# Products with the values in tiles of 64 rows by 32 columns, summed from two banks

## The chip, the cores and the metric

The kernel runs on one core of a Trainium2 chip. The metric is device time in microseconds (us), launch to end, as the median of several executions. The engines that matter here are TensorE (PE; its weight loads are shown as PEld), VectorE (DVE), ScalarE (ACT), GpSimd (POOL) and SyncE (SP), which issues most DMAs. Each engine works through its own queue in order. TensorE writes to PSUM, which has eight banks of 128 partitions by 512 float32 values; ScalarE and VectorE read the results there.

## The reference

One block of a diffusion transformer in float32, on 16 sequences of 256 tokens of width 256, with 16 heads of 16 values each:

```python
x_norm = modulate(_ln(x), shift_a, scale_a)
q, k, v = jnp.split(x_norm @ W_qkv + b_qkv, 3, axis=-1)        # 16 heads of 16
attn_w = softmax(einsum('bhqd,bhkd->bhqk', q, k) * scale, axis=-1)
attn_out = einsum('bhqk,bhkd->bhqd', attn_w, v)
x = x + gate_a * (attn_out @ W_proj + b_proj)
q_c = _ln(x) @ W_qc + b_qc                                      # cross attention,
k_c, v_c = split(_ln(context) @ W_kvc + b_kvc, 2)               # keys and values of the context
x = x + attention(q_c, k_c, v_c) @ W_cproj + b_cproj
h = gelu(modulate(_ln(x), shift_m, scale_m) @ W_mlp1 + b_mlp1)
x = x + gate_m * (h @ W_mlp2 + b_mlp2)
```

The context has 256 tokens too. The change touches the second product of each attention, weights times values (`bhqk,bhkd->bhqd`), over 256 keys.

## The kernel before

The attention is cut into 32 *units*: a self attention ("s") or a cross attention ("c") of one sequence. The first four units are s, then mostly one of each in turn. The loop at lines 1084 to 1096 goes over the units n, and inside each over eight steps k (`beat`, line 947). A step works on several units at once: while unit n has its softmax weights made, unit n+1 gets its first scores, units n+2 and n+3 get their queries, keys and values, and units n-1 to n-3 are finished. An instruction's place in its engine's queue is the place of its call in the program (`InOrder`, line 40, keeps all engines to it). After the loop comes the MLP.

One step of the loop, in PE's order:

- `visit` (line 932). Four products `s` give scores of unit n+1, with queries along the partitions; DVE takes their maxima over the keys (`mx`, `s_tile`, line 603). They go to the two banks `sp`, of which there is one pair, so the next step's `s` has to wait for this step's `mx`. Then four products `st` give the scores of unit n again, turned, with the keys along the partitions (`t_part`, line 626); ACT makes the weights `pt` from them (`exp`, line 638). Row 63 of each half holds the negative maximum, so no subtraction is needed. These products use 63 or 64 rows of the array and all 128 columns, and those of the two row halves alternate.
- In odd steps, `lanes` (line 374): two projections, interleaved product by product, one on the upper and one on the lower 64 rows. Their results lie in the long bank pair (tag "gen", two buffers).
- In even steps, what stands in `beat` for that step. Steps 0 and 4 hold what is changed here.

Step 0 (line 978) and step 4 (line 1020), in order:

- `m_part` (line 615): PE turns the maxima of one half of a unit (`psm`), ACT makes them negative (`m`), and SP sends them by DMA into row 63 of the queries, to be read four steps later.
- `exps`: ACT's exponentials of this step.
- `av_part`, twice (line 657): the products with the values, tile `o`. Each call has eight products: two chunks c of 128 keys, four heads h. A product has 128 rows (the keys) and 32 columns of the array (the 16 values of a head, then columns of ones, which give the sum of the weights), and streams 256 queries. The four heads stand in the four column strips of the array (`tile_position=(0, h * 32)`). The two calls fill one bank; then ACT copies it to `oT` in SBUF (in the last call of all, DVE does).
- then in step 4 `p1.aT.turn`: PE turns the attention output A of the unit before (`psT_a`), and ACT reads it; in step 0 nothing more on PE.
- on DVE then the low parts of keys or queries (`q2.K.low` with tile `l_k` or `l_kc`, `q2.Q.low` with `l_q` or `l_qc`), which read a bank of the long pair, and, in every second unit, statistics for a layer norm: `st_c` in step 0, `st_s` in step 4.

`psm`, `o`, `psT` and the transposed `oT` (`psA`) share the short bank pair (tag "tr", two buffers in turn, `ps_gen`, line 68). A new use of a buffer waits until all reads of the old one are done. All eight banks are given out: two `sp`, two `st`, two long, two short.

A float32 product of this kind appears in the trace as two matmul instructions.

Of the kernel before, what the change touches and what calls it, by code (L numbers as in the profile page):

```python
# [10 lines left out]
F32 = mybir.dt.float32  # L11
F32R = mybir.dt.float32r
AF = mybir.ActivationFunctionType
ALU = mybir.AluOpType
AX = mybir.AxisListType

P = 128
# [4 lines left out]
def pixart_block(  # L22
# [8 lines left out]
    B, N, H = x.shape  # L31
# [3 lines left out]
    NT = N // P  # L35
# [21 lines left out]
    PE = InOrder(nc.tensor, True)  # L57
    ACT, DVE, POOL, SP = (InOrder(e, True) for e in (nc.scalar, nc.vector, nc.gpsimd, nc.sync))

    const = ctx.enter_context(tc.tile_pool(name="const", bufs=1))  # L60
    work = ctx.enter_context(tc.tile_pool(name="work", bufs=2))
# [3 lines left out]
    LONG, SHORT = "gen", "tr"  # L65
    ps_turn = [0]

    def ps_gen(name, tag=None):


        if tag is None and ps_turn[0] is not None:
            ps_turn[0] ^= 1
            tag = (SHORT, LONG)[ps_turn[0]]
        tag = tag or SHORT
        return psum.tile([P, 512], F32, tag=tag, name=name, bufs=2)
# [314 lines left out]
    def lanes(x, y):  # L390


        if x:
            x.ps, x.fresh = ps_gen(f"ps_{x.name}", LONG), True
        return zip_longest(*(lane(o, half) for half, o in enumerate((x, y)) if o))

    def run(steps, n=12):
        for _ in islice(steps, n):
            pass
# [82 lines left out]
    def load(u):  # L482
        if u.kind == "s":
            load_x(u.b)
        else:
            u.ct = work.tile([P, NT, H], F32, tag="c", name=f"c_{u.b}")
            SP.dma_start(u.ct, tok(ctxt, u.b))
# [129 lines left out]
    def m_part(u, hf):  # L617

        pst = ps_gen(f"psm_{u.n}_{hf}", SHORT)
        PE.transpose(pst[:16, :P], u.mx[:, hf].rearrange("p r a t -> p (r a t)"), ident)  # L620
        m = work.tile([16, P], F32R, tag="m", name=f"m_{u.n}_{hf}", bufs=1)
        ACT.mul(m, pst[:16, :P], -1.0)
        for par in range(2):
            SP.dma_start(u.q[par * 64 + 63:par * 64 + 64, 4 * hf:4 * hf + 4, :].bitcast(F32),
                         m[par * 8:(par + 1) * 8].bitcast(F32))
# [19 lines left out]
    def exps():  # L645

        for f in later:
            f()
        later.clear()
# [4 lines left out]
            for f in pieces:  # L654
                next(f)

    def av_part(u, g):

        if g % 2 == 0:
            u.po = ps_gen(f"o_{u.n}_{g}", SHORT).rearrange("p (g n) -> p g n", g=2)  # L660
        for c in range(NT):
            for h in range(4):
                par, pair = g % 2, g // 2 * 4 + h
                PE.matmul(u.po[h * 32:(h + 1) * 32, g % 2], u.v[:, c, par * 8 + pair], u.pt[pair][:, par, c],
                          start=(c == 0), stop=(c == NT - 1), tile_position=(0, h * 32))
        if g % 2 == 1:
            oT = work.tile([P, 2, N], F32, tag="oT", name=f"oT_{u.n}_{g}")
            last = u.n == nu - 1 and g == 3
            (DVE.tensor_copy if last else ACT.copy)(oT.rearrange("p g n -> p (g n)"),
                                                    u.po.rearrange("p g n -> p (g n)"))  # L670
            u.oT.append(oT)


    seq = [("s", b) for b in range(4)]
# [5 lines left out]
    for n, (kind, b) in enumerate(seq):  # L680
        u = Box()
# [5 lines left out]
    nu = len(units)  # L687
# [241 lines left out]
    def unit(n):  # L929
        return units[n] if 0 <= n < nu else None  # L930

    def visit(n, k, home=sp):


        v, e = unit(n + 1), k
        s = []
        if v:
            s = [s_tile(v, e // 2, par, e % 2, par, home) for par in range(2)]
        if n < 0:
            in_turn(*s)  # L940
            return
        t = [t_part(units[n], k, par) for par in range(2)]
        in_turn(*s)
        in_turn(*t)
        later.append(lambda: exp(units[n], k))

    def beat(n, k):
        if n < 0:
            visit(n, k, (st, sp)[k % 2])
            return  # L950
        cur, prev, nxt = unit(n), unit(n - 1), unit(n + 1)
        q2, q3, q4 = (v if v and v.n >= m else None
                      for v, m in zip(map(unit, (n + 2, n + 3, n + 4)), (1, 2, 3)))
        p1, p2, p3 = (v and v.post for v in map(unit, (n - 1, n - 2, n - 3)))
        whole = n > nu - 4
        if n - 2 > nu - 5:
            p2 = None
        if n - 3 > nu - 5 or p3 and p3.hurry:
            p3 = None
        q3T = q3  # L960
        lc = q4 if q4 and q4.kind == "c" else None
        ls = q4 if q4 and q4.kind == "s" else None
        lx = q3 if q3 and q3.kind == "c" else None
        late = lx and lx.b in (0, 1, B - 2, B - 1)
        early = lc if lc and lc.b not in (0, 1, B - 2, B - 1) else None
        if k == 0 and q2:
            q2.K.high()
            q2.K.send_high()
        if k == 2 and p2:
            p2.end()  # L970
        if k == 4 and q2:
            q2.Q.high()
            q2.Q.send_high()
        if k == 6 and q2:
            q2.V.keep()
        light = k == 6 and nxt and 0 <= n < nu - 4 and not lx
        visit(n, k, (sp[:, 0], ps_gen("s1", SHORT)) if light else sp)
        if k == 0:
            if cur:
                m_part(cur, 1)  # L980
            exps()
            if prev:
                av_part(prev, 2)
                av_part(prev, 3)
            if q2:
                q2.K.low()
                q2.K.send_low()
            if p3:
                p3.add()
            if ls and n > 0:  # L990
                load(ls)
            if lc:
                lc.ln[0].steps[0]()
            if p1:
                p1.gate()
        elif k == 1:
            exps()
            run(lanes(q2 and q2.Q, p2))
            if lc:
                lc.ln[0].steps[1]()  # L1000
                lc.ln[0].steps[2]()
        elif k == 2:
            exps()
            if prev:
                p1.turn(1)
            if q3T:
                q3T.T[0].turn()
                q3T.T[0].high()
            if prev:
                p1.norm(1)  # L1010
            if p2 and p2.hurry:
                p2.add()
        elif k == 3:
            exps()
            if q3T and q3T.kind == "s":
                q3T.T[0].low()
            run(lanes(q2 and q2.V, q2 and q2.Q))
            if q3T and q3T.kind == "c":
                q3T.T[0].low()
        elif k == 4:  # L1020
            if nxt:
                m_part(nxt, 0)
            exps()
            if cur:
                av_part(cur, 0)
                av_part(cur, 1)
            if prev:
                p1.aT.turn()
                p1.aT.high()
            if q2:  # L1030
                q2.Q.low()
                q2.Q.send_low()
            if p3:
                p3.store()
            if late:
                for f in lx.ln[1].steps:
                    f()
            if ls and not late:
                ls.ln[0].steps[0]()
                ls.ln[0].steps[1](False)  # L1040
        elif k == 5:
            exps()
            run(lanes(q3 and q3.K, q2 and q2.V))
            if prev:
                p1.aT.low()
            if ls and late:
                for f in ls.ln[0].steps:
                    f()
            elif ls:
                ls.ln[0].pow()  # L1050
                ls.ln[0].steps[2]()
            if early:
                early.ln[1].steps[0]()
            v = unit(n + 5)
            if v and v.kind == "c":
                load(v)
        elif k == 6:
            exps()
            if cur:
                cur.post.begin()  # L1060
                cur.post.turn(0)
            if lx:
                lx.T[1].turn()
                lx.T[1].high()
            if early:
                early.ln[1].steps[1]()
                early.ln[1].steps[2]()
            if prev and whole:
                p1.proj(0)
                p1.proj(1)  # L1070
        elif k == 7:
            exps()
            run(lanes(None if whole else p1, q3 and q3.K))
            if prev and whole:
                p1.end()
                p1.add()
                p1.store()
            if cur:
                cur.post.norm(0)
            if lx:  # L1080
                lx.T[1].low()
# [13 lines left out]
                for f in at_end[n - nu, q]:  # L1095
                    f()
    last = units[-1]
    av_part(last, 2)
    av_part(last, 3)
    o = last.post  # L1100
    pst = iter([lambda: o.turn(1), lambda: o.norm(1),
                lambda: (o.aT.turn(), o.aT.high()), o.aT.low,
# [76 lines left out]
```

## Time and profile before

| | us |
|---|---|
| median of 3 runs | 808.84 (808.31 to 809.41) |
| span of the profiled execution | 807.9 |
| PE busy | 782.7 (97%) |
| DVE busy | 597.5 (74%) |
| ACT busy | 585.0 (72%) |
| POOL busy | 465.6 (58%) |

The first products with the values start at 46.9 us, the last end at about 612 us; from there on it is the MLP. The profiled execution's own time is known by its span, from the first to the last instruction; the measured times include what lies around it.

A row of a group gives the engine, the operation, the tiles (written <- read), the shape, the count, the busy time in us, the mean duration of one in ns, and after the second bar the engine's idle time before these instructions and what ended it. A row of the timeline gives the start in us from the start of the span, the length in us, the engine, the operation, the tiles and the count of merged instructions. Shapes of products are rows*columns of the array, then partitions x elements of what is streamed. Matmuls are pipelined: the recorded length of one is its latency, and several are under way at once. Nearly all instructions have line 51, that of a helper, so they are told apart by their tiles.

### The profile page before, as it was taken

The numbers are of one execution on the slowest core, as the hardware profiler recorded it, in microseconds if no ns is written. First come the engines' busy times: TensorE is split into PE (matmuls) and PEld (weight loads), VectorE is DVE, ScalarE is ACT, GpSimd is POOL, SyncE is SP. The second block draws the span as 40 slices with busy tenths as digits, with TensorE's granted clock in tenths as the row PEclk, the third lists the DMA queues.
The fourth block names the chain that finished last, engine by engine and source line by source line (L and its number), as shares of the span: only waits on it lengthen the run. The fifth ranks groups of instructions, "written<-read, shape, count | busy, mean of one in ns | idle before, by whom it ended". The sixth has DMA issues, their size and how long they took to land.

```text
span 807.9 us, 23702 instructions
## 1 busy us (share of the span) xinstructions
PE 782.7 (97%) x9455; PEld 659.8 (82%) x9455; DVE 597.5 (74%) x1061; ACT 585.0 (72%) x1024; POOL 465.6 (58%) x405
## 2 busy tenths in 40 slices
PE   9999999999999999999999999999889999999997
PEld 8677777878878878877777777777568999999997
DVE  4887878788887888888788888777663666566662
ACT  3367888878888888878888878887556666666663
POOL 5745737575463756636475676563435666666653
PEclk9999999999999999999999999999999999999999
DMA  6553443435344453534445453534211313312211
GB/s 201 140 166 105 122 134 111 125 99 145 106 130 110 133 136 104 146 104 128 109 126 156 124 152 109 157 94 127 88 42 41 92 50 69 79 53 67 80 41 52
DMA packets 89938, 87.88 MB, mean 109 GB/s; under 512 B 9506, under 2 KB 85572, under 8 KB 89828
## 3 DMA queue, kind: packets, MB, share of 16 engines
q1 hardware_dynamic: 89364, 85.58, 37.7%
q8 instruction: 75, 1.23, 0.6%
q0 software_dynamic: 192, 0.52, 0.2%
q14 instruction: 35, 0.29, 0.1%
q10 hardware_dynamic: 272, 0.26, 0.1%
HBM read 26.97 MB, written 8.46 MB: 44 GB/s over the span
## 4 chain that ended last, share of the span: by engine, by line
PE 73%; DVE 10%; ACT 5%; POOL 5%; issue 5%; DMA 2%; SPq 0%; POOLq 0%; ACTq 0%
PE s L51 15%; PE o L51 13%; PE ph L51 11%; PE st L51 11%; DVE mx L51 7%; PE ps_qc L51 3%; ACT pt L51 3%; PE ps_q L51 3%; PE ps_kc L51 3%; PE ps_P_s L51 2%; PE ps_v_s L51 2%; PE psm L51 1%; PE ps_v_c L51 1%; PE ps_k L51 1%; PE ps_P_c L51 1%
## 5 line engine op out<-in xcount | busy, mean ns | idle before, releaser
L51 DVE TENSOR_REDUCE mx<-s 128x4 f32<-128x1024 f32 (+1 forms) x265 | 309.1, 1171 | 96.5 <-PE s L51 93.8
L51 ACT ACTIVATE pt<-st 128x1024 f32<-128x1024 f32 x256 | 261.1, 1020 | 46.5 <-PE st L51 39.8
L51 PE MATMUL s<-big 63*128 63x256 f32 x1008 | 120.7, 309 | 9.5 <-DVE mx L51 6.4
L51 PE MATMUL o<-pt,v 128*32 128x256 f32 x2048 | 123.8, 382 | 0.0
L51 POOL TENSOR_TENSOR hl<-hf,hh 128x512 fp32r<-128x512 f32 x64 | 88.5, 1392 | 56.0 <-ACT hh L51 55.6
L51 PEld LDWEIGHTS s<-big 63*128 63x128 f32 x1008 | 80.2, 185 | 44.6 <-DVE mx L51 22.5
L51 PE MATMUL st<-big 64*128 64x256 f32 (+1 forms) x1040 | 110.7, 284 | 4.0 <-ACT pt L51 3.9
L51 PEld LDWEIGHTS o<-pt,v 128*32 128x32 f32 x2048 | 60.0, 109 | 40.8
L51 PEld LDWEIGHTS st<-big 64*128 64x128 f32 (+1 forms) x1040 | 83.4, 186 | 9.2 <-ACT pt L51 7.1
L51 ACT ACTIVATE hf<-ph,bT 128x256 f32<-128x256 f32 x120 | 50.6, 475 | 27.8 <-PE ph L51 27.8
L51 ACT ACTIVATE hh<-ph,bT 128x256 fp32r<-128x256 f32 x120 | 50.5, 472 | 24.9 <-PE s L51 13.1
L51 ACT COPY oT<-o 128x512 f32<-128x512 f32 x63 | 37.0, 587 | 42.4 <-PE o L51 42.4
L51 POOL TENSOR_TENSOR xTl_c<-y_c,xTh_c 128x512 fp32r<-128x512 f32 x16 | 20.5, 1282 | 61.1 <-PE s L51 51.9
L51 POOL TENSOR_TENSOR xTl_as<-y_as,xTh_as 128x512 fp32r<-128x512 f32 x16 | 20.5, 1279 | 57.8 <-ACT y_as L51 57.8
L51 PE MATMUL ph<-wqch,wself 128*128 128x256 f32 x256 | 51.8, 285 | 0.0
L51 PE MATMUL ph<-wkch,wself 128*128 128x256 f32 x256 | 51.8, 286 | 0.0
L51 POOL TENSOR_TENSOR xTl_ac<-y_ac,xTh_ac 128x512 fp32r<-128x512 f32 x16 | 20.5, 1281 | 54.0 <-ACT y_ac L51 50.0
L51 PE MATMUL s<-big,hh 128*128 128x256 f32 x256 | 47.4, 282 | 0.0
L51 PE MATMUL st<-big,hh 128*128 128x256 f32 x256 | 47.2, 281 | 0.0
L51 DVE TENSOR_SCALAR xn_m<-x,mv_m,rs_m 128x256 f32<-128x256 f32 x32 | 38.2, 1235 | 11.4 <-POOL rs_m L51 11.4
L51 PEld LDWEIGHTS ph<-wqch,wself 128*128 128x128 f32 x256 | 42.0, 191 | 0.4 <-issue 0.4
L51 PEld LDWEIGHTS ph<-wkch,wself 128*128 128x128 f32 x256 | 41.9, 191 | 0.4
(222 smaller groups left out, 2380.9 us busy)
## 6 DMA issues: line engine op xcount, KB each, us to landing
big<-h_kc SPq DMA_DIRECT2D x64, 128.0 KB
big<-h_qc SPq DMA_DIRECT2D x64, 128.0 KB
big<-h_k SPq DMA_DIRECT2D x62, 128.0 KB
big<-h_q SPq DMA_DIRECT2D x62, 128.0 KB
big<-l_k SPq DMA_DIRECT2D x32, 128.0 KB
big<-l_q SPq DMA_DIRECT2D x32, 128.0 KB
c<-in_ctx_dram SPq DMA_DIRECT2D x16, 256.0 KB
g<-gd SPq DMA_DIRECT2D x16, 256.0 KB
```

Of the source, the lines that this page charges most:

```text
L51: i = f(*a, **k)
```

## The change

`av_part` with its two calls becomes `av_pair`. A chunk of 128 keys is cut into two halves of 64 rows. The products of the upper half of each chunk are summed in one bank, those of the lower half in another; each product has 64 rows and 32 columns, and there are 32 calls in a block where there were 16. Both buffers of the short pair are used. On the way out ACT copies the first bank to `oT`, and DVE adds the second to it, in place. In steps 0 and 4, `exps` and `av_pair` stand ahead of `m_part`, where `m_part` came first. The call behind the loop changes likewise.

```diff
-    def av_part(u, g):
-        if g % 2 == 0:
-            u.po = ps_gen(f"o_{u.n}_{g}", SHORT).rearrange("p (g n) -> p g n", g=2)
-        for c in range(NT):
-            for h in range(4):
-                par, pair = g % 2, g // 2 * 4 + h
-                PE.matmul(u.po[h * 32:(h + 1) * 32, g % 2], u.v[:, c, par * 8 + pair], u.pt[pair][:, par, c],
-                          start=(c == 0), stop=(c == NT - 1), tile_position=(0, h * 32))
-        if g % 2 == 1:
-            oT = work.tile([P, 2, N], F32, tag="oT", name=f"oT_{u.n}_{g}")
-            last = u.n == nu - 1 and g == 3
-            (DVE.tensor_copy if last else ACT.copy)(oT.rearrange("p g n -> p (g n)"),
-                                                    u.po.rearrange("p g n -> p (g n)"))
-            u.oT.append(oT)
+    def av_pair(u, g):
+        po = [ps_gen(f"o_{u.n}_{g + i}", SHORT) for i in range(2)]
+        for a in range(2):
+            for c in range(NT):
+                for h in range(4):
+                    for half in range(2):
+                        rows, pair = slice(half * 64, half * 64 + 64), g // 2 * 4 + h
+                        PE.matmul(po[half][h * 32:(h + 1) * 32, a * N:(a + 1) * N], u.v[rows, c, a * 8 + pair],
+                                  u.pt[pair][rows, a, c], start=(c == 0), stop=(c == NT - 1),
+                                  tile_position=(half * 64, h * 32))
+        oT = work.tile([P, 2, N], F32, tag="oT", name=f"oT_{u.n}_{g + 1}")
+        flat = oT.rearrange("p g n -> p (g n)")
+        ACT.copy(flat, po[0])
+        DVE.tensor_tensor(flat, flat, po[1], ALU.add)
+        u.oT.append(oT)
...
         if k == 0:
+            exps()
+            if prev:
+                av_pair(prev, 2)
             if cur:
                 m_part(cur, 1)
-            exps()
-            if prev:
-                av_part(prev, 2)
-                av_part(prev, 3)
             if q2:
                 q2.K.low()
                 q2.K.send_low()
...
         elif k == 4:
+            exps()
+            if cur:
+                av_pair(cur, 0)
             if nxt:
                 m_part(nxt, 0)
-            exps()
-            if cur:
-                av_part(cur, 0)
-                av_part(cur, 1)
             if prev:
                 p1.aT.turn()
                 p1.aT.high()
...
     last = units[-1]
-    av_part(last, 2)
-    av_part(last, 3)
+    av_pair(last, 2)
```

## The prediction

> **What bounds the kernel now.** I read the page first, then one stretch of the loop over units (47 to 565 us), then the rows of four blocks, each a call pair of products with the values and what stands around it.
>
> ```profile
> span 807.9 us, 23702 instructions
> ...
> L51 PE MATMUL o<-pt,v 128*32 128x256 f32 x2048 | 123.8, 382 | 0.0
> ```
>
> The products with the values (tile o) are 2048 matmul instructions, two for each call, 32 for each of 64 blocks. They never wait.
>
> ```profile
> 47.00:565.00 518.00, 508.48 (x7129) 406.72 (x7126) 426.85 (x731) 422.35 (x676) 300.55 (x263) 1.00 0.45 125
> ```
>
> The columns are PE, weight loads, DVE, ACT and POOL, busy us. PE is busy for 508.48 of 518.00 us at the full clock. So in the loop a stall of PE is lost time: only 9.5 us of idle time are there to take it. DVE, with 426.85, is the second: it has some 18% free, but its maxima (tile mx) stand between one beat's scores and the next beat's, since the bank pair of the scores is single. A beat is one of the eight steps of a unit.
>
> The first block that I take as a model is step 0 of one unit. First PE, then DVE, then ACT:
>
> ```profile
> 405.53 0.41 PE L51 MATMUL s<-big 63*128 63x256 f32 x4
> 405.77 0.42 PE L51 MATMUL st<-big 64*128 64x256 f32 x4
> 406.12 0.28 PE L51 MATMUL psm<-ident,mx 128*16 128x128 f32 x1
> 406.33 1.93 PE L51 MATMUL o<-pt,v 128*32 128x256 f32 x32
> 408.19 0.51 PE L51 MATMUL s<-big 63*128 63x256 f32 x4
> ```
>
> ```profile
> 405.98 1.22 DVE L51 TENSOR_REDUCE mx<-s 128x4 f32<-128x1024 f32 x1
> 407.12 0.87 DVE L51 SCALAR_TENSOR_TENSOR l_kc<-ps_kc,bT,h_kc 128x256 fp32r<-128x256 f32 x2
> 407.91 0.74 DVE L51 BATCH_NORM_STATS2 st_c<-c 128x6 f32<-128x256 f32 x2
> 408.74 1.23 DVE L51 TENSOR_REDUCE mx<-s 128x4 f32<-128x1024 f32 x1
> ```
>
> ```profile
> 408.33 0.59 ACT L51 COPY oT<-o 128x512 f32<-128x512 f32 x1 [0.67 <-PE o L51]
> ```
>
> The reader is to see two things. PE goes from the products straight on to the scores of step 1 at 408.19, while ACT copies the result away behind its back (408.33 to 408.92): nothing on PE waits for that copy. And DVE is full between its two maxima: 407.12 to 408.65 are filled, and the next maximum starts at 408.74. A DVE operation starts some 0.08 us before the recorded end of the one before it (405.98 + 1.22 = 407.20 against 407.12).
>
> **The change part by part.**
>
> The products themselves. Each call now covers 64 rows, so there are twice as many, in eight places of the array in place of four. What a group of four costs now, and whether two row halves run side by side:
>
> ```profile
> 406.33 0.42 PE L51 MATMUL o<-pt,v 128*32 128x256 f32 x4
> ...
> 406.33 0.64 PE L51 MATMUL o<-pt,v 128*32 128x256 f32 x8
> ```
>
> ```profile
> 408.77 0.28 PE L51 MATMUL ps_qc<-xTh_q,wqch 64*128 64x256 f32 x1
> 408.78 0.28 PE L51 MATMUL ps_P_c<-wcph,xTh_ac 64*128 64x256 f32 x1
> ```
>
> Four instructions with a latency of 0.38 end within 0.42 us, so they start within 0.04 us; eight take 0.64, so a group of four costs 0.22 us in sequence (0.64 - 0.42). Two products on the two row halves start within 0.01 us of each other. Columns run side by side, and rows too. No row shows both at once; bounds are a group of eight for the price of a group of four (block 8 x 0.22, as now) and no overlap of the halves (16 x 0.22, +1.8 us a block). I take the first, nearest to both rows, plus 0.03 us a block for the longer issue. The doubled weight loads stay behind the stream as they do now. The Trainium skill, "TensorE: Matmul & The Clock Gate", section "Measured speedup vs the span model", gives one product's time plus about 4 ns a tile for row and column tiles together; by it the block's sum would be the same. No product is saved: the array was full before.
>
> The order. The transposition of the maxima (psm) goes behind the products, so the products start where psm stood, 0.21 us earlier (406.33 - 406.12). This entry still waits for st to drain: st's last product started at 405.77 + 0.42 - 0.28 = 405.91, and psm, of another shape, 0.21 later, where equal shapes follow within 0.12 (all four st start within 0.42 - 0.28 = 0.14). If 64 rows behind 64 rows need no draining, 0.1 us a block is won, 6 us in all; that end I keep for the range. The Trainium skill, "TensorEngine Tiling", section "Key Properties", says that every change of the tiling mode drains TensorE, columns too; by that the 0.21 stays as I have it.
>
> The banks. The short bank pair has two buffers. Before, psm took one and o the other, and o's idle time of 0.0 says that the other was always free by then; now o needs both 0.21 earlier, which I charge at nothing (bounds 0 and 0.21 a block). Now the two halves of the sum take both, and psm, next on PE, must wait until the copy on ACT has read the first; behind psm stand, in PE's order, all of step 1, or in step 4 the transposition of A (psT), which needs the second buffer and so the addition on DVE. The Trainium skill speaks against the change here: "TensorEngine Tiling", "PSUM Bottleneck" and "Gotcha 1: PSUM Pressure", says that tiling doesn't speed up the way out of PSUM and that row tiles need banks of their own; by it the waits below are to be expected, the sum is theirs.
>
> The addition: 128x512 on DVE, 63 in the loop. The nearest row is
>
> ```profile
> L51 DVE TENSOR_TENSOR wqcl<-xTf_m,wqch 128x512 fp32r<-128x512 f32 x7 | 4.9, 693 | 8.0 <-ACT wqch L51 8.0
> ```
>
> so 0.69 us; bounds 0.6 (the copy's 0.59) and 0.87 (the two halves of l_kc). ACT's copy stays at 0.59.
>
> One block then, counted from the old start t of psm. The copy started 2.21 after psm (408.33 - 406.12); now 2.21 - 0.21 + 0.03 = 2.03, and it ends at t + 2.62. With 0.06 for the semaphore (an estimate from o's modelled end, 406.33 + 1.93 = 408.26, and the copy's start at 408.33) psm and the addition start at t + 2.68; the addition ends at t + 3.37, and DVE is free at t + 3.29. In step 0 the scores of step 1 follow psm by 0.21: t + 2.89. In step 4 psT starts at t + 3.42.
>
> Step 0, this unit (t = 406.12). Scores of step 1 at 409.01 in place of 408.19: +0.82. But DVE was kept from l_kc, which stands behind the addition: it now runs from 409.41, takes 0.79 to the next start (407.91 - 407.12), the statistics 0.66, and the maximum of step 1 starts at 410.86, ends at 412.09. The scores of step 2 wait for that maximum: 412.14, where before they stood at
>
> ```profile
> 410.18 0.44 PE L51 MATMUL s<-big 63*128 63x256 f32 x4
> ```
>
> so +1.96. (The interleaved products of step 1 wait too, for the long bank that l_kc reads: 409.41 + 0.87 + 0.05 = 410.33, and with their 1.41, 410.18 - 408.77, end at 411.74, before 412.14.)
>
> Step 0, the other kind of unit (no statistics on DVE there):
>
> ```profile
> 388.72 0.28 PE L51 MATMUL psm<-ident,mx 128*16 128x128 f32 x1
> 388.93 1.93 PE L51 MATMUL o<-pt,v 128*32 128x256 f32 x32
> ...
> 392.78 0.43 PE L51 MATMUL s<-big 63*128 63x256 f32 x4
> ```
>
> t = 388.72: DVE is free at 392.01, l_k ends at 392.88, the interleaved products start at 392.93 and end 1.41 later; scores of step 2 at 394.34 in place of 392.78: +1.56.
>
> Step 4, first kind:
>
> ```profile
> 414.52 0.28 PE L51 MATMUL psm<-ident,mx 128*16 128x128 f32 x1
> 414.72 1.93 PE L51 MATMUL o<-pt,v 128*32 128x256 f32 x32
> 416.59 0.66 PE L51 MATMUL psT_as<-ident,A_s 128*128 128x128 f32 x4
> 417.17 0.50 PE L51 MATMUL s<-big 63*128 63x256 f32 x4
> ```
>
> psT at 414.52 + 3.42 = 417.94 in place of 416.59, +1.35; the scores follow by 0.58 as before, at 418.52. DVE has l_qc behind the addition, done by 418.68, in time for the next maximum. So +1.35.
>
> Step 4, the other kind, where DVE has statistics too:
>
> ```profile
> 397.12 0.28 PE L51 MATMUL psm<-ident,mx 128*16 128x128 f32 x1
> ...
> 399.78 0.50 PE L51 MATMUL s<-big 63*128 63x256 f32 x4
> ...
> 401.77 0.43 PE L51 MATMUL s<-big 63*128 63x256 f32 x4
> ```
>
> ```profile
> 398.93 0.74 DVE L51 BATCH_NORM_STATS2 st_s<-x 128x6 f32<-128x256 f32 x2
> 399.59 0.30 DVE L51 BATCH_NORM_AGGREGATE mv_s<-st_s 128x2 f32<-128x6 f32 x2
> ```
>
> DVE free at 400.41; l_q 0.79, statistics 0.66, aggregates 0.33, the small scalar step some 0.1: the maximum starts at 402.29, ends at 403.52; scores of step 6 at 403.57 in place of 401.77: +1.80 (PE alone would give +1.35).
>
> Sum: 1.96 + 1.56 + 1.35 + 1.80 = 6.67 us for two units. Units 2 to 27 are 13 such pairs: 86.7 us. In units 0, 1 and 28 to 31 DVE has less between its maxima; I charge PE's own waits there, 5 x 0.82 + 6 x 1.35 = 12.2 us. The 64th block, behind the loop, costs nothing: 12 products of the MLP stand before its reader. Late on SP and POOL: the DMAs of the maxima start some 2.5 us later, as psm does, but are read four steps on, and the units are themselves later; I charge nothing, and if that cover were gone PE would wait for q's row. Sum +98.9 on the profiled execution's 807.9; the median of the runs, 808.84, stands 0.9 above that span, so 907.7.
>
> **The rivals.**
>
> A: DVE makes up its delay, only PE's direct waits count: 31 x 0.82 + 32 x 1.35 = 68.6, so 877. For it: 18% of DVE is free. Against: the free time lies in odd steps, and the delay meets the next maximum at once. Chance 0.12.
>
> B: the eight places don't run together, or loads and products can't be issued at double density (128 instructions in 1.7 us, where the densest rows have 64 in 1.55, that is 1.93 - 0.38). Then a block is 1.6 to 1.8 us longer, 64 times: 102 to 115 us on top of my 908, 1010 to 1023. Nothing in the profile shows that density. Chance 0.11.
>
> C, the other side: faster. The mechanism is the draining: if 64-row tiles follow 64-row tiles with no draining, and the reordering takes the 0.21 before o away, 63 x 0.31 = 20 us are won, 789, provided the wait for the copy costs PE nothing. It decides where that wait is under 0.31 us; the rows give 0.45 to the copy's start (408.33 against a last product at 406.33 + 1.93 - 0.38 = 407.88) plus 0.59. Chance 0.04. That the sum stays within 0.2%, which is about what a measurement of this kernel tells from no change, would need a wait of just that length: 0.01.
>
> **How the numbers follow.** My case has 0.72, its own range 885 to 930: 0.1 us on each of 63 waits is 6 us, the addition between 0.6 and 0.87 gives -6 to +11, the draining -6, the buffers up to +13, the charge for the outer units 10. The range to hold eight times in ten takes in A below and stops short of B: 865 to 945. Slower holds 0.95 (mine, A, B), faster 0.04, same 0.01.
>
> **What would show it.** In the changed profile: 4096 instructions of o with a block of about 1.96 us; psm waiting for ACT's copy in 63 blocks by about 1 us; psT waiting for DVE's oT in step 4; 64 additions of about 0.69 us on DVE behind ACT's copy; scores waiting longer for mx; PE's idle time up by about the 99 us. The prediction is wrong if psm starts within 0.3 us of the last product, if the block of o lasts over 2.5 us, or if scores wait for DVE no more than now.

## The result and the profile after

The changed kernel takes 913.3 us (median of 4 runs, 910.48 to 914.11) against 808.58 us in the same series: a ratio of 1.1276, 95% interval 1.1249 to 1.1302. The prediction was 908, 865 to 945, slower.

The page of the changed kernel (a group's row: count, then busy us and mean ns, then the engine's idle time before it and what ended it):

```profile
span 911.2 us, 27905 instructions
...
L51 PE MATMUL o<-pt,v 64*32 64x256 f32 x4096 | 128.2, 379 | 0.1
...
L51 DVE TENSOR_TENSOR oT<-oT,o 128x512 f32<-128x512 f32 x64 | 44.0, 688 | 99.0 <-ACT oT L51 99.0
...
L51 PEld LDWEIGHTS psm<-ident,mx 128*16 128x16 f32 x64 | 5.6, 87 | 74.6 <-ACT oT L51 74.3
```

Twice as many products take 128.2 us where they took 123.8. So the products are not where the time went. There are two new waits: DVE stands 99.0 us in front of its 64 additions until ACT's copy is there, and TensorE's weight loads stand 74.3 us in front of psm for the same copy. They run at the same time, so they don't add up; and a part of the second passes while the last products are still under way. PE's own idle time there is shorter (us in total, times, longest):

```profile
PE psm L51 <- ACT oT L51: 44.5, 62, 0.7
```

Units 2 to 27 by the windows view, before and after, from step 0 of unit 2 to step 0 of unit 28 (columns as before: PE, weight loads, DVE, ACT, POOL):

```profile
73.64:530.46 456.82, 449.26 (x6354) 360.88 (x6353) 379.75 (x655) 376.52 (x602) 267.90 (x234) 1.00 0.45 125
```

```profile
80.01:622.10 542.09, 469.59 (x8019) 383.56 (x8017) 406.33 (x707) 385.47 (x603) 267.53 (x234) 1.00 0.39 106
```

These units take 85.3 us more (542.09 - 456.82). PE has 72.5 us of idle time there (542.09 - 469.59), where it had 7.6 (456.82 - 449.26). The other 20.3 us of the loss are recorded as busy. A product is recorded with its whole latency, so the ends of the products ahead of a wait are likely the most of it; no run takes that apart.

Eight products at once, from a timeline cut to their first 0.06 us:

```profile
299.11 0.45 PE L51 MATMUL o<-pt,v 64*32 64x256 f32 x8
```

With a latency of 0.38 us each (379 ns above), eight that end within 0.45 us have started within 0.07. Row halves and column strips do run side by side.

A block of step 0, the kind of unit with statistics on DVE, PE first and then DVE:

```profile
309.92 2.05 PE L51 MATMUL o<-pt,v 64*32 64x256 f32 x64
312.67 0.28 PE L51 MATMUL psm<-ident,mx 128*16 128x128 f32 x1 [0.70 <-ACT oT L51]
312.87 0.50 PE L51 MATMUL s<-big 63*128 63x256 f32 x4
...
315.96 0.50 PE L51 MATMUL s<-big 63*128 63x256 f32 x4
```

```profile
309.80 1.22 DVE L51 TENSOR_REDUCE mx<-s 128x4 f32<-128x1024 f32 x1
312.64 0.69 DVE L51 TENSOR_TENSOR oT<-oT,o 128x512 f32<-128x512 f32 x1 [1.62 <-ACT oT L51]
313.25 0.87 DVE L51 SCALAR_TENSOR_TENSOR l_kc<-ps_kc,bT,h_kc 128x256 fp32r<-128x256 f32 x2
314.04 0.74 DVE L51 BATCH_NORM_STATS2 st_c<-c 128x6 f32<-128x256 f32 x2
314.69 1.21 DVE L51 TENSOR_REDUCE mx<-s 128x4 f32<-128x1024 f32 x1
```

The products now start where psm stood, so 309.92 is the prediction's t. The scores of step 1 come 2.95 after it (before: 408.19 - 406.12 = 2.07), those of step 2 come 6.04 after it (before: 410.18 - 406.12 = 4.06). DVE shows why the second delay is larger: it idles 1.62 us in front of the addition, and l_kc, the statistics and the maximum of step 1 come behind it, one against the other without a gap.

A block of step 4:

```profile
320.36 2.08 PE L51 MATMUL o<-pt,v 64*32 64x256 f32 x64
323.15 0.28 PE L51 MATMUL psm<-ident,mx 128*16 128x128 f32 x1 [0.71 <-ACT oT L51]
323.78 0.66 PE L51 MATMUL psT_as<-ident,A_s 128*128 128x128 f32 x4 [0.36 <-ACT m L51]
324.37 0.50 PE L51 MATMUL s<-big 63*128 63x256 f32 x4
```

psm starts 2.79 and psT 3.42 after the block's start. psT doesn't wait for the addition, as the prediction had it, but for ACT's m, which reads psm. ACT and DVE at that place:

```profile
323.46 0.27 ACT L51 ACTIVATE m<-psm 16x128 fp32r<-16x128 f32 x1 [0.37 <-PE psm L51]
```

```profile
323.13 0.69 DVE L51 TENSOR_TENSOR oT<-oT,o 128x512 f32<-128x512 f32 x1 [1.66 <-ACT oT L51]
```

m ends at 323.73, the addition at 323.82, when psT is already under way. The trace's semaphores (the counters by which engines wait for each other) say the same: in step 4 of units 1 to 30, psT's first weight load waits for the counter that ACT raises, and m ended each of these waits; the addition raised DVE's counter only after psT had started, in 29 of the 30 by 0.04 to 0.05 us. So psT got the bank that psm had just used, not the second one.

### The profile page after: what moved, and what is told of

Read it like the earlier page. It is cut to its first block, busy times and chain, and to the rows that moved or that the text cites. A ratio compares the mean times of both kernels' runs of the same rounds, so it can differ in the third digit from the quotient of the medians.

```text
span 911.2 us, 27905 instructions
## 1 busy us (share of the span) xinstructions
PE 808.6 (89%) x11503; PEld 689.4 (76%) x11503; DVE 631.4 (69%) x1124; ACT 595.3 (65%) x1025; POOL 465.9 (51%) x405
## 4 chain that ended last, share of the span: by engine, by line
PE 62%; DVE 18%; ACT 9%; issue 8%; POOL 4%; DMA 0%; POOLq 0%; ACTq 0%; DVEq 0%
PE o L51 13%; PE s L51 13%; DVE mx L51 10%; PE st L51 9%; PE ph L51 9%; ACT oT L51 4%; PE ps_q L51 3%; ACT pt L51 3%; PE ps_kc L51 2%; PE ps_P_s L51 2%; PE ps_qc L51 2%; DVE l_kc L51 2%; DVE l_k L51 1%; PE ps_v_s L51 1%; PE psT_as L51 1%
## 5 line engine op out<-in xcount | busy, mean ns | idle before, releaser
L51 PE MATMUL o<-pt,v 64*32 64x256 f32 x4096 | 128.2, 379 | 0.1
L51 DVE TENSOR_TENSOR oT<-oT,o 128x512 f32<-128x512 f32 x64 | 44.0, 688 | 99.0 <-ACT oT L51 99.0
L51 PEld LDWEIGHTS s<-big 63*128 63x128 f32 x1008 | 77.9, 186 | 44.2 <-DVE mx L51 32.1
L51 PEld LDWEIGHTS o<-pt,v 64*32 64x32 f32 x4096 | 86.0, 106 | 20.2 <-PE st L51 0.3
L51 PEld LDWEIGHTS psm<-ident,mx 128*16 128x16 f32 x64 | 5.6, 87 | 74.6 <-ACT oT L51 74.3
L51 PE MATMUL psm<-ident,mx 128*16 128x128 f32 x64 | 17.7, 277 | 44.5 <-ACT oT L51 44.5
```

Of the source, the lines that this page charges most:

```text
L51: i = f(*a, **k)
```

## The experiments

My theory: the loss is made of waits for the two short banks, on PE directly, and on DVE through the addition that stands in its queue. Rivals: the 64-row tiles themselves, the new order by itself, or DVE's additional load.

| | us, median | ratio to before, 95% |
|---|---|---|
| the change | 913.3 | 1.1249 to 1.1302 |
| order alone | 822.59 | 1.0168 to 1.0209 |
| tiles alone, old order | 951.07 | 1.1726 to 1.1837 |
| the change without the addition | 832.4 | 1.0282 to 1.0318 |
| the change, addition last on DVE in step 0 | 881.37 | 1.0896 to 1.0929 |
| the change, everything that waited put later | 844.38 | 1.0421 to 1.046 |
| the same order, old products | 824.4 | 1.0184 to 1.0223 |
| old products, maxima two steps later | 845.69 | 1.0456 to 1.0503 |
| everything put later, without the addition | 832.92 | 1.0229 to 1.0312 |

**Order alone.** The old products, ahead of `m_part`, in step 4 as in step 0:

```diff
         if k == 0:
-            if cur:
-                m_part(cur, 1)
             exps()
             if prev:
                 av_part(prev, 2)
                 av_part(prev, 3)
+            if cur:
+                m_part(cur, 1)
...
```

> The products as before (128 rows, one bank, one copy), but ahead of the maxima's transposition as in the change. My theory (the waits for two banks make the loss): in step 0 nothing is lost, psm finds the other buffer free; in step 4 psT now needs the bank of o and waits for ACT's copy, about 0.6 us in 32 blocks: 827 us (820 to 835). If the new order by itself made the loss (the maxima come late): about 910. If the tiles made it: about 808, unchanged.

Measured 822.59, in my range. The order makes a seventh of the loss, and where the theory puts it: in step 4 psT wants the bank of o and stands 0.50 us for ACT's copy.

```profile
282.44 0.28 PE L51 MATMUL psm<-ident,mx 128*16 128x128 f32 x1
283.21 0.66 PE L51 MATMUL psT_as<-ident,A_s 128*128 128x128 f32 x4 [0.50 <-ACT oT L51]
```

**Tiles alone.** The change with `m_part` back in front of `exps` and `av_pair`, in step 4 as in step 0.

```diff
         if k == 0:
+            if cur:
+                m_part(cur, 1)
             exps()
             if prev:
                 av_pair(prev, 2)
-            if cur:
-                m_part(cur, 1)
...
```

> The new products, two banks and the addition, but with the maxima's transposition ahead of them as before the change. My theory: slower than the change, since the second bank must now wait for ACT to read psm (products end about 0.7 us later), and DVE's addition with all that stands behind it comes 0.7 us later; 2.65 and 2.25 us in the two kinds of step 0, 1.4 and 2.5 in step 4, 933 us (915 to 950). If the new order made the loss: near 815.

Measured 951.07: the order is not what loses; with the tiles it saves 38 us, of which the clock (last section) may be up to 12. A block of step 0:

```profile
347.47 0.28 PE L51 MATMUL psm<-ident,mx 128*16 128x128 f32 x1
347.68 2.43 PE L51 MATMUL o<-pt,v 64*32 64x256 f32 x64
350.04 0.50 PE L51 MATMUL s<-big 63*128 63x256 f32 x4
...
352.33 0.38 PE L51 MATMUL ps_q<-xTh_s,wself 64*128 64x256 f32 x1 [1.55 <-DVE l_k L51]
```

The products last 2.43 in place of 1.96 us, for their second bank is psm's, and the interleaved products of step 1 stand 1.55 us for l_k, which stands behind the addition on DVE. The median lies 1 us above my range.

**Without the addition.**

```diff
         ACT.copy(flat, po[0])
-        DVE.tensor_tensor(flat, flat, po[1], ALU.add)
```

> The change without the addition: the half of the keys in the second bank is left out of the result. All matmuls, both banks and ACT's copy stay. My theory: psm's wait for the copy stays (0.82 us in 31 steps 0), in step 4 psT comes right behind psm (0.78 us in 32), and DVE's queue is delayed no more: 859 us (850 to 870). If the matmuls in 64-row tiles made the loss: about 910, as with the change. If DVE's load alone made it: about 810.

Measured 832.4, 27 us below what I expected, so one of my steps was wrong. psm no longer waits for the copy (us in total, times, longest):

```profile
PEld psm L51 <- PE o L51: 38.7, 62, 0.6
```

```profile
287.94 0.28 PE L51 MATMUL psm<-ident,mx 128*16 128x128 f32 x1
288.51 0.66 PE L51 MATMUL psT_as<-ident,A_s 128*128 128x128 f32 x4 [0.30 <-ACT oT L51]
```

It waits for the products' own end, 0.6 us at most, and psT then for the copy. I read from this that psm was given the second bank, which nobody reads in this kernel, and not the first in turn, as I had assumed: the bank that comes free first. What the run shows of the addition alone is therefore an upper bound: 81 us with it and with the longer hold of a bank that it brings.

The runs so far are steps from the kernel before to the change: the order 14.5 us (822.59 against 808.12 in that series), the new products in that order 9.8 more (832.4; PE idles 5.0 of it in front of psm until the products end), the addition with its hold of the bank 80.9 more (913.3). So the tiles themselves aren't free, but they are only a tenth of the loss.

**The addition last on DVE in step 0.** All is kept; only DVE's order in step 0 is changed: `prev.add` is the tensor_tensor of `av_pair`, kept until there.

```diff
             if lc:
                 lc.ln[0].steps[0]()
+            if prev:
+                prev.add()
```

> The change, but in step 0 DVE has the addition behind the low part of the keys and the statistics, so these no longer stand behind its wait for ACT's copy. My theory: step 0 then costs only PE's wait for the copy, 0.82 us in place of 1.96 and 1.56: 24 us less than the change, 889 us (882 to 896). If DVE's order doesn't matter (PE's direct waits alone): 913, unchanged.

Measured 881.37, 32 us less than the change and 0.6 us below my range. DVE in step 0, to be set against the rows above:

```profile
297.57 0.87 DVE L51 SCALAR_TENSOR_TENSOR l_kc<-ps_kc,bT,h_kc 128x256 fp32r<-128x256 f32 x2
298.35 0.74 DVE L51 BATCH_NORM_STATS2 st_c<-c 128x6 f32<-128x256 f32 x2
299.27 0.69 DVE L51 TENSOR_TENSOR oT<-oT,o 128x512 f32<-128x512 f32 x1 [0.18 <-ACT oT L51]
300.04 1.22 DVE L51 TENSOR_REDUCE mx<-s 128x4 f32<-128x1024 f32 x1
```

The wait in front of the addition falls from 1.62 to 0.18 us; the copy's delay is covered by work that DVE has to do anyway. So about a third of the loss was not the wait itself but what stood behind it. PE's wait in front of psm is as long as in the change (44.5 us). Of the 30.5 us between the two profiled spans (911.2 - 880.7), 26.0 lie in units 2 to 27, about what I had expected there; 4.5 lie in the other units, where I had expected nothing.

**Everything that waited put later,** and the same order with the old products. psm goes behind the interleaved products of steps 1 and 5, the transposition of A into step 5 behind st, the addition behind DVE's other work in both steps. The lines are taken out of steps 0 and 4 in return; in step 4 `cur.add()` comes last.

```diff
         elif k == 1:
             exps()
             run(lanes(q2 and q2.Q, p2))
+            if cur:
+                m_part(cur, 1)
...
         elif k == 5:
             exps()
+            if prev:
+                p1.aT.turn()
+                p1.aT.high()
             run(lanes(q3 and q3.K, q2 and q2.V))
             if prev:
                 p1.aT.low()
+            if nxt:
+                m_part(nxt, 0)
...
```

> The new products with two banks and the addition, with everything that waited for the banks put later: psm behind the interleaved products of steps 1 and 5, the transposition of A in step 5 behind st, the addition on DVE behind the low parts and statistics. My theory: the products and the addition themselves cost nearly nothing, so nearly all of the 105 us is gone; what stays is more changes of shape on PE (0.12 us in step 0, 0.25 in step 4) and the banks' late entry (0.1): 822 us (812 to 835). If the 64-row products or DVE's extra 44 us cost time by themselves: 850 or more.

> The same order as in the run before this one, with the products as they were (128 rows, one bank, no addition). My theory: the same changes of shape, so within 5 us of it: 819 us (810 to 830). If the tiles or the addition have a price of their own that the order hides nowhere, this one is at 820 and the other far above it.

Measured 844.38 and 824.4. Of the 105 us, 69 are gone with the waits, so they were the bulk, and the old products land where I put them. But the new ones stay 20 us above, out of my range and short of the 850 that I had put against it: they do have a price left in this order. DVE in step 0 of the run with the new products, and then of the run with the old ones:

```profile
281.70 0.74 DVE L51 BATCH_NORM_STATS2 st_c<-c 128x6 f32<-128x256 f32 x2
282.62 0.69 DVE L51 TENSOR_TENSOR oT<-oT,o 128x512 f32<-128x512 f32 x1 [0.18 <-PE st L51]
283.23 1.22 DVE L51 TENSOR_REDUCE mx<-s 128x4 f32<-128x1024 f32 x1
```

```profile
274.70 0.74 DVE L51 BATCH_NORM_STATS2 st_c<-c 128x6 f32<-128x256 f32 x2
275.36 1.21 DVE L51 TENSOR_REDUCE mx<-s 128x4 f32<-128x1024 f32 x1
```

From the statistics' start to the maximum's it is 1.53 us with the addition, 0.66 without; the scores of step 2 wait for that maximum. So I removed the addition, in both steps:

```diff
-        add = lambda: DVE.tensor_tensor(flat, flat, po[1], ALU.add)
+        add = lambda: None
```

> The run in which everything that waited was put later (new products), now without the addition, so the half of the keys in the second bank is left out of the result. If what stayed there above the old products in the same order (844 against 824 us) is the addition, which on DVE pushes the maximum of step 1 back: 828 us (823 to 833). If it is the 64-row products and their banks: 840 or more.

Measured 832.92 (828.99 to 834.24), at the upper end of my range. The addition, with the wait in front of it and the bank that it holds, on a DVE that is full in that step, is thus 11 of the 20 us. Of the 9 that remain, about as many as in the first order (9.8), the products' groups account for 4.3 (busy time of o, 128.1 in that run against 123.8); the clock fell to half for 6.8 us in the profiled executions of both new-product runs, which is up to 3.4. That these two are all of the rest is argued, not shown.

**Maxima two steps later.** The run with an eye on a faster kernel: the old products, psm taken out of steps 0 and 4 and put beside the transpositions of steps 2 and 6.

```diff
         elif k == 2:
             exps()
+            if cur:
+                m_part(cur, 1)
...
         elif k == 6:
             exps()
+            if nxt:
+                m_part(nxt, 0)
...
```

> The kernel before, with only the maxima's transposition moved two steps later, next to the transpositions of steps 2 and 6, whose shape it shares. My theory: in 64 blocks one change of shape (0.2 us) goes and 0.1 us for psm stays in the other place: 802 us (798 to 808), faster by 0.8%. If the DMA of the maxima, now only two steps ahead of its reader, comes too late: slower, 815 or more.

Measured 845.69, far from my range, and slower. The rival that I had named allowed for that, but the cause is mostly another. PE and ACT in a step 2:

```profile
278.60 0.28 PE L51 MATMUL psm<-ident,mx 128*16 128x128 f32 x1
278.72 0.60 PE L51 MATMUL psA_s<-ident,oT 128*128 128x128 f32 x4
279.99 0.66 PE L51 MATMUL psT_q<-ident,xn_q 128*128 128x128 f32 x4 [0.68 <-ACT m L51]
```

```profile
278.77 1.02 ACT L51 ACTIVATE pt<-st 128x1024 f32<-128x1024 f32 x1
279.69 0.25 ACT L51 ACTIVATE m<-psm 16x128 fp32r<-16x128 f32 x1
```

The DMA of the maxima is named for 2.9 us of PE's idle time in all, in front of st; ACT's m is named for 30.2 in front of psT (11.2, 10.8 and 8.2 for psT_q, psT_c and psT_s), of the 37 us lost. It is the bank pair once more. psm, psA and psT want two buffers one behind the other, psT stands for ACT's reading of psm, and that stands behind the exponential. Three users in a row, 0.68 us of PE's time lost here, as in step 4 of the change. No version here beats the kernel before.

## Why the prediction was right

**The products.** Taken at the price of before plus 0.03 us a block, on rows that showed row halves and column strips side by side only one at a time. Right: 128.2 against 123.8 us, 0.07 us a block. The 0.03 were the longer issue. The rest lies in about half of the blocks, between the first product and the second, which goes to the second bank: the block at 309.92 lasts 2.05 us, the one at 299.11, shown next, 1.96. I had charged the banks' entry at nothing with 0.21 as its bound; that the second bank comes late there is argued, not shown. Rival B, no overlap or no issue at that density, is out.

```profile
299.11 1.96 PE L51 MATMUL o<-pt,v 64*32 64x256 f32 x64
```

**The draining at the entry.** Kept at 0.21, and it stays:

```profile
298.76 0.42 PE L51 MATMUL st<-big 64*128 64x256 f32 x4
```

st's last product started at 298.76 + 0.42 - 0.28 = 298.90, the first o 0.21 later, at 299.11. So 64 rows behind 64 rows cost as much here, where the columns change. The Trainium skill, "TensorEngine Tiling (Array Packing)", section "Key Properties", says that a change of the tiling mode drains TensorE; the trace agrees. The end of my range that had 6 us won there is out, and so is rival C's mechanism.

**The four terms.** By the starts of the scores, counted from t, the typical block (median) of units 2 to 27:

| | predicted | measured |
|---|---|---|
| step 0, with statistics | 6.02, +1.96 | 6.04, +1.98 |
| step 0, without | 5.62, +1.56 | 5.71, +1.65 |
| step 4, first kind: scores of step 5 | 4.00, +1.35 | 4.00, +1.35 |
| step 4, other kind: scores of step 6 | 6.45, +1.80 | 6.40, +1.75 |

The rows of the second and fourth, for the starts at 330.53 and 299.11:

```profile
330.53 1.96 PE L51 MATMUL o<-pt,v 64*32 64x256 f32 x64
...
336.24 0.42 PE L51 MATMUL s<-big 63*128 63x256 f32 x4
```

```profile
305.51 0.51 PE L51 MATMUL s<-big 63*128 63x256 f32 x4 [0.32 <-DVE mx L51]
```

Their sum is 6.73 where I had 6.67. Units 2 to 27 lose 85.3 us where I had 86.7; units 24 to 26 lose less than the typical ones, about 1.27 us in step 4. That the delay on DVE counts, and not PE's direct waits alone (rival A, 877), the run with the addition last shows: 32 us hang on DVE's order in step 0.

**Where it fell short.** The profiled spans differ by 103.3 us (911.2 - 807.9), my sum was 98.9. The mis-sized term is the one of the outer units, 0, 1 and 28 to 31: charged 12.2, what is left for them is 103.3 - 85.3 = 18.0. I had given them PE's own waits alone, 0.82 us in step 0, with DVE free. DVE isn't free there: the scores of step 2 come 2.08 us later in unit 1, and 1.70 and 1.69 in units 28 and 29. The run with the addition last on DVE in step 0 loses 4.5 us less in the outer units, which is most of the 5.8 that I had missed; up to 1.7 of the 4.5 is the clock (last section), which falls there in the change and not in that run.

**Right, but with a wrong step.** "Two buffers in turn", as the kernel's description and the prediction have it, was not how banks are given out, as the run without the addition showed. In the change psm got the first bank either way, since that comes free first. But psT didn't get the second bank and didn't wait for the addition: it waited for ACT's m. The two ways out, copy and addition on one side, copy, psm and m on the other, end within 0.1 us of each other, so psT started at 3.42 as predicted. The +1.35 of step 4, first kind, is thus luck: the size held and the reason didn't.

Of the other signs that I had named, most are there: 4096 instructions of o in blocks of 1.96 to 2.08 us, psm's wait in 62 blocks, 64 additions of 0.69 us, and more waiting for mx (9.2 us of PE's idle time in front of s, where it was 6.4). PE's idle time is up by 77 us and not by 99 (911.2 - 808.6 busy, against 807.9 - 782.7).

## What to carry to other kernels

When a change takes a second buffer of a pair, ask who has the next use of it on the same in-order engine, and count the whole way out: last product, copy, second pass. An operation that must wait for another engine's copy should stand in its queue behind work that is ready: here that alone was worth 32 us of 105. And an array that four column strips already fill had nothing to gain here from eight smaller tiles (128.2 against 123.8 us); what they add is a second way out. A prediction's time can be right while one of its waits is for another engine than it says, so read in the trace whom each wait was for.

## What the runs showed beside that

The clock. No row of the kernel before has less than the full clock in the loop. With the new waits it falls to half for 3.4 or 6.8 us at a time, without any long idle stretch of PE. The changed kernel once, and the run with the tiles alone (its longest wait of PE in the stretch ahead is one of 1.56 us for l_kc, of the kind shown above for l_k), with the 3.4 us that go ahead:

```profile
60.80:64.20 3.40, 2.46 (x23) 2.13 (x25) 3.37 (x9) 1.29 (x2) 0.00 (x0) 1.00 0.30 80
64.20:67.60 3.40, 3.40 (x22) 2.85 (x24) 2.06 (x4) 1.57 (x3) 3.07 (x3) 0.51 0.27 74
```

```profile
371.90:375.30 3.40, 1.84 (x34) 1.34 (x22) 2.33 (x6) 1.61 (x2) 2.60 (x3) 1.00 0.40 109
375.30:378.70 3.40, 3.40 (x29) 3.18 (x26) 2.48 (x5) 1.52 (x2) 1.93 (x3) 0.50 0.31 82
```

In the stretch ahead PE was busy for 2.46 and 1.84 of 3.40 us. The Trainium skill, "TensorE: Matmul & The Clock Gate", section "HAM oscillation — how this bites in real kernels", gives the rule of no idle gap above about 3.4 us. Here half the clock comes after waits of 1.6 us at most, so a gap of that length isn't needed for it. Whether the share of busy time decides stays open: the tiles-alone run has 29 waits of 1.55 or 1.56 us, and the clock falls about 1 us behind four of them alone. In that run about 24 us lie at half the clock, up to 12 us of the time; its four executions took from 947.41 us, at a mean granted clock of 0.995, to 957.78 at 0.979.
